# Smaller broadcasts of C in a fused Mamba and local-attention kernel: four 2 KB tiles with their own lead beside five 4 KB tiles for B

## The chip, the core and the metric

The kernel runs on one NeuronCore of one Trainium2 chip. A core has engines that run at the same time, each through its own list of instructions in the order in which the program was written: TensorE (PE, with its weight loads PEld), VectorE (DVE), ScalarE (ACT), GpSimd (POOL) and SyncE (SP), which here does nothing but issue DMAs. Engines wait for one another by semaphores. The metric is device time in microseconds of the whole kernel; lower is better.

## What is computed

The input x is 4096 tokens of 256 features. Two branches start from it and their results are added to x.

- A Mamba block: project the normalised x to 512 channels twice (x_inner and a gate z), a causal convolution of 4 taps and silu on x_inner, then a selective scan with 16 states for each channel, and an output projection.
- A local transformer of two layers: attention over windows of 128 tokens that also look at the window before, 8 heads of 64, and a gated MLP of width 682.

The part that the change touches is the scan. For each channel d, state n and token l:

```
dt  = softplus(dt_lr @ dt_proj_w.T + dt_proj_b)
dA  = exp(dt[d] * A[d, n])
dBx = dt[d] * x_conv[d] * B_ssm[l, n]
h   = dA * h + dBx
y  += h * C_ssm[l, n]
```

B_ssm and C_ssm are rows of 16 states that are the same for all channels. Everything is in 32-bit floats.

## The kernel before

Channels lie on the 128 partitions and tokens along the free axis. The Mamba branch goes in 8 blocks of 512 tokens (`NB`), each with 4 groups of 128 channels (`CI`) and 16 states; the transformer branch goes in 16 steps of 256 tokens (`ST`) for each of the two layers. Both are interleaved through the whole kernel: 32 MLP steps stand beside 32 pairs of block and channel group.

`recur(b, c, g)` (from L775) handles two states (`NG = 2`) of one block and channel group; there are 256 such calls, 512 states in all. In the kernel before, one call

- takes two tiles of the pool `spreads` (L381: 7 tiles, 128 x 1024, 4 KB in each partition) and issues for each a DMA of 512 KB that broadcasts two rows of B, or two rows of C, from DRAM to all 128 partitions;
- multiplies the B tile, u, by dt*x on POOL (L793), one instruction of 1024 columns for both states;
- for each state: ACT makes the decay exp(dt*A) in one of two PSUM tiles (L802), DVE scans (L807), ACT keeps the last column as state (L813), DVE multiplies the scan by the row of C into u (L817);
- in every second call POOL adds the two states (L825), and PE transposes the result and sums it in PSUM (L829, tile y). When all 16 states are in, `close` copies y (L846), turns it back (L850), and DVE and POOL finish the channel group (L854, L859).

So the tile u is held from its DMA until PE has read it, and the C tile from its DMA until the second product on DVE.

The block's front comes earlier: `in_proj` (PE, L635), a copy and a scaled copy on ACT (L665, L672), three taps for each channel group on DVE (L678), silu, the small projection `front_dbl` (PE L702, result to DRAM by SP), then `times` (PE L734) and `prepare` (the softplus on ACT, DVE and POOL, L742 to L770).

In the transformer branch `load_rest` brings the MLP weights of a layer. It lets PE make a bias out of them (`shift`, L495), and DVE adds that bias (L506, L507) and scales the weights (L511). An MLP step ends with the gelu on ACT (L1213, with a table load on each side), products on POOL (L1221), and the down projection on PE (L1247 in layer 0, L1266 in layer 1). `finish` adds the result to a tile of sums (L546).

What sets the order is a planner in the kernel itself. Each `add` records an operation with its engine, a supposed duration and a lead, `soon`; a lower key (time wanted less `soon`) goes first. `Plan.order` plays the operations through and writes every engine's instructions in the order that comes out. Once written, the order is fixed: an instruction that is not ready holds up all that stand behind it on its engine, DMA issues on SP among them. PE's `part` tells whether a matmul uses the whole array, row halves (`rows`) or column halves (`columns`).

Of the kernel before, what the change touches and what calls it, by code (L numbers as in the profile page):

```python
# [42 lines left out]
AHEAD = 2.32  # L43
# [275 lines left out]
def mamba_and_local_transformer(  # L319
# [61 lines left out]
    spreads = buffer("bc", 7, [P, NG, TB])  # L381
# [73 lines left out]
    def load_small():  # L455
        dma(96, lambda: xpw.ap, lambda: xp_wT.rearrange("(c p) n -> p c n", p=P), writes=[xpw], soon=-0.84)
        for at_row in (0, DH):
            dma(32, lambda at_row=at_row: dtw.ap[at_row : at_row + DTR], lambda: dt_wT, writes=[(dtw, at_row)], soon=-0.13)
        dma(128, lambda: b2row.ap, lambda: b2_d[DEPTH - 1 : DEPTH, :].partition_broadcast(P), writes=[b2row], soon=-0.82)

    def load_qkv(l):
        for s in range(3):
            cut = slice(s * INNER, (s + 1) * INNER)
            dma(
                512, lambda cut=cut: wqkv.ap[:, :, cut],
                lambda cut=cut: wqkv_d[l][:, cut].rearrange("(k p) n -> p k n", p=P), writes=[(wqkv, s)], soon=-0.17,
            )

    def load_rest(l):
        dma(512, lambda: wo.ap, lambda: wo_d[l].rearrange("(h p) n -> p h n", p=P), writes=[wo], soon=0.41)  # L470
        for half in range(2):
            for m, n in ((0, WHOLE), (NM - 1, LAST)):
                to, of = w1_at(half, m), half * HID + m * MC
                dma(
                    n, lambda to=to, n=n: w1.ap[:, :, to : to + n],
                    lambda of=of, n=n: w1_d[l][:, of : of + n].rearrange("(k p) n -> p k n", p=P),
                    writes=[(w1, (half, m))], soon=-1.5,
                )
# [3 lines left out]
            lambda: w2_d[l][0:whole, :].rearrange("(m p) n -> p m n", p=MC), writes=[(w2, 0)], soon=0.34,  # L482
        )
        dma(42, lambda: w2.ap[0 : HID - whole, NM - 1, :], lambda: w2_d[l][whole:HID, :], writes=[(w2, 1)], soon=0.91)
# [28 lines left out]
        add("PE", 8.3, shift, [w1], [pb], soon=-0.76)  # L513
        add("DVE", 0.4, bias, [pb], [b1, b1x], soon=-0.11)
        add("DVE", 4.6, scale, [], [w1], port=True, soon=-1.45)
# [14 lines left out]
    def base_of(s):  # L530

        base = plan.value(rows_b)
        if s in sums:
            dma(256, lambda: base.ap, lambda: sums[s].ap, [sums[s]], [base], soon=-0.77)
            return base
        dma(256, lambda: base.ap, lambda: rows(x, s), writes=[base], soon=-1.13)
# [3 lines left out]
            ), [b2row], [base], soon=-0.58,  # L540
# [3 lines left out]
    def finish(s, po, base):  # L544

        add("DVE", 0.6, lambda: nc.vector.tensor_tensor(base.ap, halves(po), base.ap, ALU.add), [po], [base], soon=-1.06)  # L546
        if s in sums:
            dma(256, lambda: rows(out, s), lambda: base.ap, [base], soon=-0.55)
            return
        sums[s] = plan.fixed(dram.tile([P, NW, D], F32, tag=f"sum{s}", name=f"sum{s}"))  # L550
        dma(256, lambda: sums[s].ap, lambda: base.ap, [base], [sums[s]], soon=-1.4)
# [4 lines left out]
    def shift_column(l, s):  # L556
        now = xts[l, s]
        if s == 0:
            add("POOL", 0.14, lambda: nc.gpsimd.memset(now.ap[:, 1, 0:1], 0.0), [], [(now, 0)], soon=-0.51)
        else:  # L560
# [3 lines left out]
                [(old, 1)], [(now, 0)], soon=-0.73,  # L564
            )

    def normalize(s):
# [5 lines left out]
        dma(256, lambda: xb.ap, lambda: rows(x, s), writes=[xb], soon=0.15)  # L573
# [27 lines left out]
        add("DVE", 1.1, stats, [xb], [mv], soon=1.5)  # L601
        add("ACT", 0.5, root, [mv], [rstd], soon=0.26)
        add("DVE", 0.6, centre, [mv, rstd], [xb], port=True, soon=0.02)
        now = xts[0, s] = plan.value(tokens)
        add("PE", 0.44, turn, [xb], [pt], holds=[now], soon=0.92)
        add("ACT", 0.48, lambda: nc.scalar.copy(now.ap[:, :, 1:], halves(pt)), [pt], [(now, 1)], soon=0.26)
        shift_column(0, s)
        dma(256, lambda: xn_d[s].ap, lambda: now.ap[:, :, 1:], [(now, 1)], [xn_d[s]], soon=0.98)
# [3 lines left out]
    def reload(s):  # L612
        now = xts[1, s] = plan.value(tokens)
        dma(256, lambda: now.ap[:, :, 1:], lambda: x1_d[s].ap, [x1_d[s]], [(now, 1)], soon=0.04)
# [6 lines left out]
    def in_half(i):  # L621
# [3 lines left out]
            lambda: in_wT[:, i * DI : (i + 1) * DI].rearrange("(k p) n -> p k n", p=P), writes=[w], soon=-1.17,  # L625
# [3 lines left out]
    def in_proj(b, w, c, to):  # L629
# [9 lines left out]
        add("PE", 1.72, emit, [w, xms[b]], [pm], holds=[to], soon=-0.68)  # L639
        return pm  # L640

    def front_load(b):
        xm = xms[b] = plan.value(xms_b)
        for i in range(PB):
            s = b * PB + i
            dma(
                256, lambda i=i: xm.ap[:, :, i * TS : (i + 1) * TS], lambda s=s: xn_d[s].ap, [xn_d[s]], [(xm, i)], soon=0.54
# [5 lines left out]
    def front_conv(b, c, w):  # L653
# [4 lines left out]
        else:  # L658
# [3 lines left out]
                [(old, c)], [(xin, 0)], soon=0.95,  # L662
            )
        pm = in_proj(b, w, c, xin)
        add("ACT", 0.48, lambda: nc.scalar.copy(xin.ap[:, TAPS - 1 :], pm.ap), [pm], [(xin, 1)], soon=1.39)  # L665
        if b < NB - 1:
            add(
                "POOL", 0.14, lambda: nc.gpsimd.tensor_copy(tail.ap[:, edge], xin.ap[:, TB:]), [(xin, 1)], [(tail, c)], soon=-0.13
# [5 lines left out]
            ), [], [pm], soon=-1.0,  # L674
# [8 lines left out]
        for j in range(TAPS - 1):  # L683
            add("DVE", 0.7, lambda j=j: tap(j), [xin, pm], [(xc, c) if j == TAPS - 2 else pm], soon=1.04)

    def silu(v):
# [4 lines left out]
        add("ACT", 4.52, emit, [], [v], soon=0.84)  # L691

    def front_dbl(b):
# [3 lines left out]
        def emit():  # L697
# [9 lines left out]
        add("PE", 1.75, emit, [xc, xpw], [px], holds=[xd, part], soon=-0.37, part="columns")  # L707
        add("ACT", 0.48, lambda: nc.scalar.copy(part.ap[0:n, 0:TB], px.ap[DH : DH + n]), [px], [part], alone=[px], soon=-0.04)
        add(
            "DVE", 0.6, lambda: nc.vector.tensor_tensor(xd.ap[0:n], px.ap[0:n], part.ap[0:n, 0:TB], ALU.add),  # L710
            [px, part], [(xd, 0)], alone=[px], soon=-1.5,
        )

        add("ACT", 0.48, lambda: nc.scalar.copy(xd.ap[DH : DH + DTR], xd.ap[0:DTR]), [(xd, 0)], [(xd, 1)], soon=-0.52)
        xds[b] = xd
        bc = bcs[b] = plan.fixed(dram.tile([2 * NS, TB], F32, tag=f"bc{b}", name=f"bc{b}"))
        dma(64, lambda: bc.ap, lambda: xd.ap[DTR:n, :], [(xd, 0)], [bc], soon=-0.16)

    def gate_conv(b, c, w):
# [4 lines left out]
        add("ACT", 0.48, lambda: nc.scalar.copy(sz.ap[:, c, :], pz.ap), [pz], [(sz, c)], soon=-1.5)  # L724

    def times(b, c):
# [12 lines left out]
        add("PE", 1.15, emit, [xd, dtw], banks2, holds=dts2, soon=1.25, part="rows")  # L739
        for i in range(2):  # L740
# [3 lines left out]
                ), [banks2[i]], [dts2[i]], soon=0.16,  # L744
# [3 lines left out]
    def prepare(b, c):  # L748

        if c % 2 == 0:  # L750
# [7 lines left out]
        add("ACT", 0.6, lambda: nc.scalar.activation(e.ap[:, n], dt.ap, AF.Abs), [dt], [e], soon=-0.49)  # L758
        add("ACT", 0.6, lambda: nc.scalar.activation(dt.ap, dt.ap, AF.Relu), [], [dt], soon=-1.5)
        add("ACT", 0.54, lambda: nc.scalar.activation(e.ap[:, n], e.ap[:, n], AF.Exp, scale=-1.0), [], [e], soon=0.5)  # L760
        add(
            "DVE", 0.36, lambda: nc.vector.tensor_scalar(r.ap[:, n], e.ap[:, n], 1.0, -1.0, ALU.add, ALU.add),
            [e], [r], port=True, soon=-0.19,
        )
        add("POOL", 1.22, lambda: nc.gpsimd.tensor_tensor(r.ap[:, n], e.ap[:, n], r.ap[:, n], ALU.subtract), [e], [r], soon=-0.36)
        add("ACT", 0.6, lambda: nc.scalar.activation(e.ap[:, n], e.ap[:, n], AF.Ln, bias=one_t), [], [e], soon=-0.3)
        add("POOL", 1.22, lambda: nc.gpsimd.tensor_tensor(dt.ap, dt.ap, r.ap[:, n], ALU.add), [r], [dt], soon=-1.41)
        add("POOL", 1.22, lambda: nc.gpsimd.tensor_tensor(dt.ap, dt.ap, e.ap[:, n], ALU.add), [e], [dt], soon=-0.94)
        add(
            "DVE", 0.61, lambda: nc.vector.tensor_tensor(dtx.ap, dt.ap, xc.ap[:, c, :], ALU.mult),  # L770
            [dt, (xc, c)], [dtx], port=True, soon=0.7,
# [3 lines left out]
    def recur(b, c, g):  # L775
# [5 lines left out]
        spread = []  # L781
        for s in range(2):
            w = plan.value(spreads)
            dma(
                512, lambda w=w: w.ap.rearrange("p n t -> p (n t)"),
# [636 lines left out]
```

## Time and profile before

| What | Value |
|---|---|
| Median of three runs | 1888.05 us (1886.05 to 1889.43) |
| Profiled execution, its own time | 1890.55 us |
| Its span, first to last instruction | 1888.8 us |
| Mean granted TensorE clock | 0.992 of full speed |
| First matmul starts, last matmul ends | 7.51 us, 1884.84 us |
| Matmul records | 12,432 |
| DMA issues on SP that broadcast B or C | 512 of 512 KB each |

Shares and waits are taken from this one profiled execution. The page counts an engine as busy while any of its instructions runs; matmuls overlap in the pipeline and their ends are modelled, so PE's busy share says little about how much room is left. The distance from one matmul's start to the next one's start says more. In the lists of waits, the columns are the total in microseconds, the number of waits, and the longest.

### The profile page before, as it was taken

To read this page: it belongs to the slowest core of one execution; us is meant where nothing else is said; L and a number is where in the kernel's file an instruction comes from. 1 tells how busy PE (TensorE), PEld (TensorE's weight loads), DVE (VectorE), ACT (ScalarE), POOL (GpSimd) and SP (SyncE) were. 2 spreads that over 40 slices of the span, in tenths; PEclk is the share of its full clock that TensorE was granted. 3 is DMA by queue.
4 is the path that set the end of the run, shared out by engine and by line. 5 is a ranking of instruction groups with operands and counts; after the bars stand their busy time and mean duration, and the time that the engine had idled before them with its cause. 6 is when DMAs were issued, how large, how long until landed. Compare 5 with 4: busy or idle time off the path is not lost. (4 is left out here: it accounts for less than half of the span.)

```text
span 1888.8 us, 35786 instructions
## 1 busy us (share of the span) xinstructions
PE 1850.9 (98%) x12432; PEld 1422.4 (75%) x12432; DVE 1667.1 (88%) x3030; ACT 1588.7 (84%) x3794; POOL 1508.6 (80%) x1274
## 2 busy tenths in 40 slices
PE   7999999999999999999999999999999999999997
PEld 4777767777777777778778787787778777787886
DVE  6688898899898999988899888989889898899886
ACT  5788888888898888897896979988798888988793
POOL 4578778887887778887888787988788987798885
PEclk9899999999999999999999999999999999999999
DMA  5354555565455555556555554556544575455564
GB/s 189 125 193 131 171 167 167 178 209 179 157 176 190 181 179 185 164 186 208 166 186 204 181 191 147 187 170 209 176 147 171 176 248 169 144 173 175 193 197 142
DMA packets 133956, 334.69 MB, mean 177 GB/s; under 512 B 13468, under 2 KB 57200, under 8 KB 133776
## 3 DMA queue, kind: packets, MB, share of 16 engines
q1 hardware_dynamic: 133488, 332.21, 53.1%
q8 instruction: 98, 1.61, 0.3%
q14 instruction: 82, 0.67, 0.1%
q10 hardware_dynamic: 288, 0.20, 0.0%
HBM read 315.06 MB, written 17.30 MB: 176 GB/s over the span
## 5 line engine op out<-in xcount | busy, mean ns | idle before, releaser
L793 POOL TENSOR_TENSOR bc<-dtx,bc 128x1024 f32<-128x1024 f32 x256 | 605.7, 2368 | 80.7 <-DMA bc<-bc 44.7
L807 DVE TENSOR_TENSOR_SCAN da<-da,state,bc 128x512 f32<-128x512 f32 x448 | 563.7, 1279 | 56.6 <-ACT da L802 32.8
L802 ACT ACTIVATE da<-dt,negA 128x512 f32<-128x512 f32 x512 | 349.2, 698 | 49.7 <-DVE bc L817 47.9
L918 PE MATMUL mm<-wqkv,xt 128*128 128x512 f32 x768 | 353.5, 598 | 1.4 <-DVE top L1032 0.8
L817 DVE TENSOR_TENSOR bc<-da,bc 128x512 f32<-128x512 f32 x512 | 338.3, 679 | 5.8 <-ACT state L813 3.7
L1176 PE MATMUL mm<-hn,w 128*128 128x256 f32 (+1 forms) x1408 | 329.2, 381 | 2.1 <-DVE top L1032 0.7
L1176 PEld LDWEIGHTS mm<-hn,w 128*128 128x128 f32 (+1 forms) x1408 | 256.1, 188 | 39.1 <-DVE top L1032 1.6
L1042 ACT ACTIVATE pr<-pr,top 128x256 f32<-128x256 f32 (+1 forms) x512 | 253.3, 501 | 10.6 <-DVE top L1032 10.4
L918 PEld LDWEIGHTS mm<-wqkv,xt 128*128 128x128 f32 x768 | 139.7, 191 | 137.0 <-issue 121.2
L1032 DVE CUSTOM_DVE_ANT_0 pr<-mm,maskf,nrm 128x256 f32<-128x256 f32 (+1 forms) x512 | 212.4, 473 | 14.5 <-PE mm L1017 13.7
L825 POOL TENSOR_TENSOR bc<-bc 128x512 f32<-128x512 f32 x128 | 165.3, 1291 | 71.5 <-DVE bc L817 65.2
L829 PE MATMUL y<-ident,bc 128*128 128x128 f32 x1536 | 219.6, 277 | 2.2 <-ACT m2k L846 1.5
L985 POOL TENSOR_TENSOR turn<-turn,trig 128x512 f32<-128x512 f32 x128 | 162.4, 1288 | 74.0 <-DVE turn L978 63.0
L829 PEld LDWEIGHTS y<-ident,bc 128*128 128x128 f32 x1536 | 177.1, 141 | 58.6 <-issue 40.0
L945 POOL TENSOR_TENSOR turn<-turn,turn 128x512 f32<-128x512 f32 x128 | 164.2, 1283 | 32.4 <-DVE turn L965 31.4
L1017 PEld LDWEIGHTS mm<-kT,qT 64*128 64x128 f32 x2016 | 119.7, 187 | 30.9 <-issue 21.9
L1221 POOL TENSOR_TENSOR mlp<-mlp,ga 128x512 f32<-128x512 f32 (+2 forms) x128 | 127.2, 1008 | 19.1 <-ACT ga L1233 10.0
L1059 ACT COPY prT<-mm 128x512 f32<-128x512 f32 (+1 forms) x256 | 133.9, 595 | 3.4 <-PE mm L1055 3.1
L1017 PE MATMUL mm<-kT,qT 64*128 64x128 f32 x2016 | 135.4, 280 | 0.0
L1071 PE MATMUL mm<-prT,v 128*64 128x128 f32 x2016 | 134.5, 281 | 0.0
L1071 PEld LDWEIGHTS mm<-prT,v 128*64 128x64 f32 x2016 | 113.8, 137 | 25.1 <-issue 8.8
L1055 PE MATMUL mm<-ident,pr 128*128 128x128 f32 x1008 | 130.5, 276 | 2.0 <-ACT qT L956 0.9
(132 smaller groups left out, 3499.4 us busy)
## 6 DMA issues: line engine op xcount, KB each, us to landing
bc<-bc SPq DMA_DIRECT2D x512, 512.0 KB, 4.5
io<-in_x SPq DMA_DIRECT2D x32, 256.0 KB, 5.4
mw<-in_in_wT SPq DMA_DIRECT2D x16, 512.0 KB, 4.8
rot<-in_rot SPq DMA_DIRECT2D x32, 128.0 KB, 4.2
xn<-xt SPq DMA_DIRECT2D x16, 256.0 KB, 3.6
xm<-xn SPq DMA_DIRECT2D x16, 256.0 KB, 4.4
x<-mid SPq DMA_DIRECT2D x16, 256.0 KB, 4.6
mw<-in_out_wT SPq DMA_DIRECT2D x8, 512.0 KB, 6.1
```

The lines of the kernel that those rows point to most:

```text
L793: "POOL", 2.35, lambda: nc.gpsimd.tensor_tensor(u.ap, dtx.ap.unsqueeze(1).to_broadcast([P, NG, TB]), u.ap, ALU.mult), [dtx], [u], soon=-0.28,
L802: "ACT", 0.63, lambda h=h, n=n: nc.scalar.activation(h.ap, dt.ap, AF.Exp, scale=negA[:, c * NS + n : c * NS + n + 1]), [dt], [h], soon=0.0,
L807: "DVE", 1.18, lambda h=h, n=n, i=i: nc.vector.tensor_tensor_scan(h.ap, h.ap, u.ap[:, i, :], state.ap[:, c, n : n + 1] if b else 0.0, ALU. ...
L817: "DVE", 0.61, lambda h=h, i=i: nc.vector.tensor_tensor(u.ap[:, i, :], h.ap, spread[1].ap[:, i, :], ALU.mult), [h, spread[1]], [(u, i)], a ...
L825: add("POOL", 1.22, lambda: nc.gpsimd.tensor_tensor(u.ap[:, 0, :], u.ap[:, 0, :], u.ap[:, 1, :], ALU.add), [], [u], soon=-1.1)
L829: nc.tensor.matmul(y.ap[:, t, :], lhsT=u.ap[:, i, t * P : (t + 1) * P], rhs=ident, is_transpose=True, start=g == 0 and i == 0 and t == 0, ...
L918: nc.tensor.matmul(pm.ap, lhsT=hT[k], rhs=wqkv.ap[:, k, q * INNER : (q + 1) * INNER], start=k == 0, stop=k == KC - 1,)
L1017: nc.tensor.matmul(halves(scs[j])[:, i, a * WIN : (a + 1) * WIN], lhsT=qT.ap[half, 2 * g + i, :], rhs=kk.ap[half, 2 * g + i, :], start=n == 0,
L1032: nc.vector.tensor_tensor_reduce(out=prs[j].ap[:, i, keys], in0=halves(scs[j])[:, i, keys], in1=mask[:, keys], scale=nrm.ap[:, h : h + 1], ...
L1042: nc.scalar.activation(prs[j].ap[:, i, keys], prs[j].ap[:, i, keys], AF.Exp, bias=top.ap[:, h : h + 1], scale=-1.0, accum_out=den.ap[:, h ...
L1071: nc.tensor.matmul(hpair(po.ap)[j * DH : (j + 1) * DH, hp, :], lhsT=vv.ap[:, h * DH : (h + 1) * DH], rhs=prT.ap[:, j, a, :], start=a == first,
L1176: nc.tensor.matmul(halves(pm)[0:r, i, :], lhsT=w1.ap[:, k, c0 : c0 + r], rhs=hn.ap[:, k, :], start=k == 0, stop=k == KC - 1,)
```

## The change

The pool `spreads` shrinks from seven tiles to five and serves B alone. A new pool `readouts` of four tiles of 128 x 512 (2 KB in each partition) serves C. A call of `recur` issues one DMA of 512 KB for B and, for each of its two states, one DMA of 256 KB for C. The bytes in SBUF (28 KB in each partition) and the bytes moved stay as they were. The leads `soon` of nearly all operations, and the planner's horizon `AHEAD`, have other values; the DMA of B now has the lead -0.14 and that of C -1.5, where both had -0.76. No operation of an engine other than SP is added or taken away, but the order of the instructions on every engine is another one.

```diff
-AHEAD = 2.32
+AHEAD = 2.34
...
-    spreads = buffer("bc", 7, [P, NG, TB])
+    spreads = buffer("bc", 5, [P, NG, TB])
+    readouts = buffer("cc", 4, [P, TB])
...
-        add("PE", 8.3, shift, [w1], [pb], soon=-0.76)
-        add("DVE", 0.4, bias, [pb], [b1, b1x], soon=-0.11)
-        add("DVE", 4.6, scale, [], [w1], port=True, soon=-1.45)
+        add("PE", 8.3, shift, [w1], [pb], soon=-1.41)
+        add("DVE", 0.4, bias, [pb], [b1, b1x], soon=0.06)
+        add("DVE", 4.6, scale, [], [w1], port=True, soon=0.25)
...
         y, bc = ys[b, c], bcs[b]
-        spread = []
-        for s in range(2):
-            w = plan.value(spreads)
-            dma(
-                512, lambda w=w: w.ap.rearrange("p n t -> p (n t)"),
-                lambda s=s: bc.ap.rearrange("(s n) t -> s n t", s=2)[s, g * NG : (g + 1) * NG, :]
-                .rearrange("n t -> (n t)").partition_broadcast(P), [bc], [w], soon=-0.76,
-            )
-            spread.append(w)
-
-        u = spread[0]
+        rows_of = lambda s, n, k: bc.ap.rearrange("(s n) t -> s n t", s=2)[s, n : n + k, :].rearrange("n t -> (n t)").partition_broadcast(P)
+        u = plan.value(spreads)
+        dma(512, lambda: u.ap.rearrange("p n t -> p (n t)"), lambda: rows_of(0, g * NG, NG), [bc], [u], soon=-0.14)
...
         for i in range(NG):
             n = g * NG + i
+            cc = plan.value(readouts)
+            dma(256, lambda cc=cc: cc.ap, lambda n=n: rows_of(1, n, 1), [bc], [cc], soon=-1.5)
...
-                "DVE", 0.61, lambda h=h, i=i: nc.vector.tensor_tensor(
-                    u.ap[:, i, :], h.ap, spread[1].ap[:, i, :], ALU.mult
-                ), [h, spread[1]], [(u, i)], alone=[h], soon=-0.32,
+                "DVE", 0.61, lambda h=h, i=i, cc=cc: nc.vector.tensor_tensor(
+                    u.ap[:, i, :], h.ap, cc.ap, ALU.mult
+                ), [h, cc], [(u, i)], alone=[h], soon=-0.25,
...
-        add("ACT", 0.48, lambda: nc.scalar.copy(ytv(), y.ap), [y], [yt], soon=-0.43)
+        add("ACT", 0.48, lambda: nc.scalar.copy(ytv(), y.ap), [y], [yt], soon=-0.7)
...
-        add("PE", 0.44, turn, [yt], [py], soon=-0.55)
+        add("PE", 0.44, turn, [yt], [py], soon=0.51)
...
-        add("ACT", 4.1, gelu, [], [u], soon=-1.49)
+        add("ACT", 4.1, gelu, [], [u], soon=-1.33)
```

## The prediction

> **What bounds the kernel now.** I read the page first, then the chain of waits, the stages, the lists of waits, and the two ends of the timeline.
>
> ```profile
> span 1888.8 us, 35786 instructions
> ...
> PE 1850.9 (98%) x12432; PEld 1422.4 (75%) x12432; DVE 1667.1 (88%) x3030; ACT 1588.7 (84%) x3794; POOL 1508.6 (80%) x1274
> ```
>
> PE at 98% may only mean that matmuls overlap. The chain tells what PE needs at full pace, where matmuls follow one another without a wait:
>
> ```profile
> 1665.33 3.57 PE mm L1112 x32
> 1669.33 1.73 PE mm L1176 x8
> ...
> 1678.83 1.72 PE mm L918 x4
> ...
> 1693.96 1.95 PE mm L1071 x32
> ...
> 1701.24 1.99 PE mm L1017 x32
> ```
>
> Per matmul this is 430 ns for 512 columns, 216 for 256, 111 for 128 (109 where weights don't change), 61 where two halves of the array work at once (L1071; 56 for L1017 by its starts). The instruction counts times these: 1024 x 0.43 = 440, 2560 x 0.216 = 553, 4592 x 0.1095 = 503, 2016 x 0.0555 = 112, 2016 x 0.061 = 123, small forms 39: near 1,766 us with unrounded starts. So 118 us of PE's time up to its last matmul (1884.84) are lost, and the change keeps all 12,432 matmuls. Where is it lost? Setting each matmul's start against the sum of work before it: 7.6 us before the first; 19.2 us at 39 us of work; 23.8 at 61; 46.9 at 300; 107.5 at 1750; 118.3 at the end. From 300 to 1750 it is 60.6 us in 1450, 4.2 in 100, of which most is inherent: of 1,313 changes from one group of matmuls to the next, 1,076 cost under 0.1 us and 27 us in all, and each turn to the row halves about 0.2. I put true waits there at 10 us. What a better order can win lies at the ends:
>
> ```profile
> 0.00:300.00 300.00, 280.81 (x1824) 203.97 (x1825) 244.72 (x485) 241.68 (x582) 212.42 (x214) 0.98 0.50 163
> 300.00:600.00 300.00, 298.41 (x1992) 228.28 (x1991) 278.12 (x517) 259.58 (x643) 248.79 (x207) 1.00 0.53 175
> ...
> 1800.00:1889.00 89.00, 76.20 (x506) 65.92 (x504) 63.89 (x89) 54.89 (x113) 61.74 (x43) 0.95 0.52 172
> ```
>
> PE (first column after the length) is idle for 19 us in the first stage, 13 in the last, 1.6 between. What the tiles of B and C do stands in the waits:
>
> ```profile
> POOL bc L793 <- DMA bc<-bc: 44.7, 33, 3.6
> ...
> DVE da L807 <- POOL bc L793: 12.6, 10, 4.2
> ```
>
> POOL waits 44.7 us for B. No line shows DVE's second product (L817) waiting for C. Following every tile from its DMA to its last reader: B is used a median 1.4 us after it lands, C 9.4 us after; B is held 29.7 us on average (median), C 17.8. A call of recur comes every 1889/256 = 7.38 us, so seven tiles offer 51.6 us and are filled for 47.5: C's slack is bought with B's.
>
> **The change part by part.** *B's tiles.* Five tiles for B alone offer 5 x 7.38 = 36.9 us against 29.7 held, so B can be asked for some 7 us earlier and most of the 44.7 us go. They are POOL's; POOL has 20% idle, and only 12.6 us reach the scan. On PE, waits that POOL ends cost 17 us in all, 9 of them at the end of the kernel. So I take -4.5, between 0 (all hidden) and -10.
>
> *C's tiles.* A tile is free when DVE has ended L817 and is used again four states later. In the new program DVE's own work between the two, at the durations of this trace, is at least 5.8 us, below 7 in 5 of 508 cases, below 8 in 25, with a median of 12.5. Landings: 4.5 us for the 512 KB, 4.4 for 256 KB from DRAM (xm<-xn); the slowest tenth of the broadcasts took over 6.2 us, the slowest 10. Before, SP issued within 0.1 us of the tile's release in nine of ten cases, though its queue is in order and nearly always waits (DVE 645 us, PE 499 us), so releases come in the order in which the DMAs stand. About one use in forty is late by about 1 us: 13 us on DVE, which has 12% idle: +0.5, between 0 and +3. Behind a late C wait the next scans, POOL's sum and PE's collection.
>
> *More DMAs.* 256 more issues at 0.32 us are 82 us of SP, which waits more than 1,500 us: nothing, while releases stay in order. [...] I take the trace: 0.
>
> *The start.* In both programs the first block's chain is conv, silu, L702, L734, softplus, first scan, first collection (L829). Before:
>
> ```profile
> 51.64 6.87 PE L495 MATMUL mm<-cols,w 128*128 128x1 f32 x48
> ...
> 58.44 2.08 PE L734 MATMUL mm<-xd,dtw 16*128 16x512 f32 x4
> ...
> 84.56 1.09 PE L829 MATMUL y<-ident,bc 128*128 128x128 f32 x8
> ```
>
> The bias matmuls stand right ahead of L734, whose input was ready at 52.1: it lost 6 us; and from L734 to the first collection it took 24 us, with POOL serving the second channel group's softplus first. The new program has L495 at 15.6 us of PE work (33.8 before), L734 at 41.9 (39.2) and the first collection at 58.1 (60.9); POOL goes straight from the first softplus to L793. New on the chain: the bias and scale of the weights (0.5 + 1.8 us by L506 to L511) stand ahead of the taps on DVE. L495 now needs w1 early: its DMAs come after some 5.1 MB, and 6.2 MB had moved by 22 us before, so it lands near 19, ahead of the 27 to 29 at which PE gets there. I get L734 at 56 to 58, and the chain to the collection needs at least 13 us by its rows (ACT 3 x 0.63, DVE 0.43 + 0.66, POOL 1.38 + 1.27 + 1.27 + 2.37, scans and product 3.1, signals) and more with company, 15 to 18: at 73 to 76, with 58.1 of work done, 15 to 18 us lost where 23.8 were. I take -6, between -10 and +2 (chain as slow as before).
>
> *The end.* Before:
>
> ```profile
> 1857.20 1.28 ACT L1213 ACT_TABLE_LOAD   x1
> ...
> 1862.38 2.47 DVE L807 TENSOR_TENSOR_SCAN da<-da,state,bc 128x512 f32<-128x512 f32 x2 [2.56 <-ACT da L802]
> ...
> 1866.19 2.46 DVE L807 TENSOR_TENSOR_SCAN da<-da,state,bc 128x512 f32<-128x512 f32 x2 [0.16 <-ACT da L802]
> ...
> 1871.32 0.69 DVE L817 TENSOR_TENSOR bc<-da,bc 128x512 f32<-128x512 f32 x1
> ```
>
> After the last gelu begins ACT still has 5 decays to make; two states take 3.81 us, and from the gelu to the last product it is 14.8 us, then 17 us of closing that stay. The new ACT list has 7 decays there: +3.81; three short copies instead of one stand ahead of the first decay: +0.75; and L546 (0.69) stands ahead of the last product: 5.3 in all. PE comes to this gelu with one collection less done (-0.44): +5, between +2 and +7.
>
> *Tighter hand-offs.* The new PE list puts less work between steps that depend on one another through ACT: between the last collection of a channel group and its transposes (L850), under 2.5 us in 12 of 32 groups (2 before); between turning the softmax and mixing (L1055, L1071), under 1.25 us in 19 of 128 (6 before). Without cover the first costs PE 0.84 us (at 1873.5), the second about 0.3 (L1071 waits 6.4 us in 29 for ACT). Most still have 0.9 us or more between: +2, between 0 and +13. Turns between array parts fall from 361 to 351, at 0.1 to 0.2 each: -1.
>
> Sum: -4.5 + 0.5 - 6 + 5 + 2 - 1 = -4. The profiled execution took 1890.55 (1.75 outside its span), so 1886.5 there; the median of the runs is 2.5 lower: 1884.
>
> **The rivals.** *The hand-offs decide, slower:* ACT is 84% busy and works in order, so a copy behind exps or a gelu (4.1 us) comes late, and PE with its fixed list stands. 10 closes at 0.8 and 13 mixes at 0.4 are 13 instead of 2: +7, 1895. It turns the sign from 6 us on. For it: PE has nothing else to do at such a place. Against it: before, such places cost little. *The start heals further:* from 61 to 300 us of work PE lost 23 us, 9.7 in 100; at the later rate it would be 10: 13 less, 1871. For it: B's tiles run short there too. Against it: these waits are on DVE's attention steps. *It does nothing on PE:* B's waits were covered (0), the start gives 3 and the end takes 5: 1889.
>
> **How the numbers follow.** The likeliest, 1884 (own range 1878 to 1890), has 0.47; the hand-offs 0.30; the healed start 0.13; nothing 0.10. A measurement tells about 0.2%, 3.8 us: faster is below 1884.3, slower above 1891.8. Of the likeliest 0.26 is faster, 0.16 same, 0.05 slower; of the hand-offs 0.29 slower; of nothing 0.06 same, 0.02 each side. With the healed start: faster 0.41, same 0.23, slower 0.36. The range leaves out half of the healed start and the hand-offs at their worst: 1872 to 1898.
>
> **What would show it.** Right: POOL's wait for B under 15 us, no wait of L817 for C above 15 us in all, the first collection before 77 us, the last product 19 to 21 us after the last gelu begins, PE's loss from 300 to 1750 us of work between 55 and 62. Wrong: L817 waiting long for cc (C late), L495 waiting for w1, the first collection after 82 us, or a new list of PE waits for ACT at L850 and L1071 of over 8 us.

## The result and the profile after

| | Before | After |
|---|---|---|
| Median on the same chip | 1888.74 us (1886.05 to 1891.51) | 1913.3 us (1911.62 to 1918.26) |
| Ratio, 95% interval | | 1.0134 (1.0110 to 1.0158) |
| Profiled execution, span | 1888.8 us | 1909.8 us |
| Granted TensorE clock | 0.992 | 0.989 |
| PE's time lost, start to last matmul | 118.3 us | 139.3 us |

The change costs 25 us where a gain of 4 was forecast. The last row is counted as in the prediction: each matmul's start less the work that stands before it. The page of the profile after:

```profile
span 1909.8 us, 36533 instructions
...
PE 1859.5 (97%) x12432; PEld 1427.1 (75%) x12432; DVE 1689.1 (88%) x3030; ACT 1589.3 (83%) x3794; POOL 1505.7 (79%) x1274
```

These are the same matmuls and DVE instructions as before, but DVE is busy 22 us longer. Where PE stands still shows first in the table by stages; of before:

```profile
300.00:1000.00 700.00, 695.66 (x4665) 533.57 (x4664) 644.28 (x1184) 609.58 (x1488) 574.79 (x480) 1.00 0.55 181
1000.00:1800.00 800.00, 798.24 (x5443) 618.96 (x5441) 714.20 (x1275) 682.59 (x1615) 659.65 (x540) 1.00 0.54 180
```

and of after (columns: the stretch, then busy time of PE, PEld, DVE, ACT, POOL, then the clock, the DMA share, GB/s):

```profile
300.00:1000.00 700.00, 685.96 (x4622) 525.47 (x4621) 642.47 (x1142) 597.34 (x1448) 561.79 (x473) 1.00 0.55 176
1000.00:1800.00 800.00, 799.72 (x5441) 621.42 (x5438) 718.01 (x1280) 682.58 (x1628) 656.53 (x539) 0.99 0.56 181
```

From 300 to 1000 us, the transformer's first layer, PE idles 14 us instead of 4; from 1000 to 1800 the two are alike. By work done: up to 61 us of work PE has lost 23.7 us (23.8 before); from 61 to 300, 24.0 (23.1); from 300 to 1000, 50.2 (33.9); from 1000 to 1750, 26.2 (26.7); behind that 15.2 (10.8). So of the 21 us, 16.3 fall in layer 0 and 4.4 at the end.

The waits of POOL in the profile after:

```profile
POOL turn L981 <- DVE turn L974: 96.2, 33, 7.4
...
POOL bc L787 <- DMA bc<-bc: 43.2, 31, 4.5
```

The wait for B, which five own tiles were to take away, is still there: 43.2 us, 44.7 before. The new order asks for the tiles so that each is held 36.1 us (median), which is all that five tiles offer (5 x 1909.8/256 = 37.3). And POOL waits half as long again for DVE's rotation (96.2 us; 63.0 before, at L985).

No wait of PE names a DMA of B or C as what ended it. Two places in layer 0 show what does, both of after. The first:

```profile
371.06 1.28 ACT L689 ACT_TABLE_LOAD   x1
...
372.36 1.91 ACT L689 ACTIVATE sz<-sz 128x2048 f32<-128x2048 f32 x1
...
374.29 1.28 ACT L690 ACT_TABLE_LOAD   x1
374.42 0.60 PE L1051 MATMUL mm<-ident,pr 128*128 128x128 f32 x4
...
376.34 1.08 ACT L1055 COPY prT<-mm 128x512 f32<-128x512 f32 x2
...
377.08 0.63 PE L946 MATMUL mm<-ident,turn 128*128 128x128 f32 x4 [2.06 <-ACT prT L1055]
```

PE turns the softmax (L1051) and next needs a bank that ACT empties (L1055). ACT is inside a silu with a table load on each side, 4.5 us, and does two small steps more; PE, whose list is fixed, stands 2.06 us. And more is lost than this wait. Right behind it the granted clock (the third number from the end) is at half for 3.4 us:

```profile
377.90:381.30 3.40, 3.40 (x10) 2.69 (x9) 2.14 (x4) 3.37 (x13) 0.07 (x1) 0.51 0.06 23
381.30:384.70 3.40, 3.40 (x27) 2.69 (x27) 1.81 (x3) 1.81 (x6) 3.40 (x4) 1.00 0.08 30
```

The 13 matmuls of 256 columns that follow (L875) take 4.66 us, where 13 x 0.216 = 2.8 would do. A second spell of 3.4 us at half clock stands behind waits of 1.66 and 0.66 us, from 968.4 us on. In before, neither is there. The second place:

```profile
647.13 3.48 DVE L590 TENSOR_SCALAR io<-io,mv,rstd 128x256 f32<-128x256 f32 x2
...
648.11 4.69 POOL L787 TENSOR_TENSOR bc<-dtx,bc 128x1024 f32<-128x1024 f32 x2
...
650.52 1.28 DVE L803 TENSOR_TENSOR_SCAN da<-da,state,bc 128x512 f32<-128x512 f32 x1
...
652.64 1.38 PEld L1172 LDWEIGHTS mm<-hn,w 128*128 128x128 f32 x7 [2.92 <-DVE top L1028]
652.64 1.56 PE L1172 MATMUL mm<-hn,w 128*128 128x256 f32 x6 [2.51 <-DVE top L1028]
```

Two normalisations on DVE (L590), at most 0.41 us each in the ten cases in which POOL does nothing beside them, take 3.48 us while POOL works, mostly on B; the masks (L1028) behind them are late, and PE stands 2.5 us. (No half clock follows here: it is 1.00 from 652 to 660 us, as it is behind a wait of 1.25 us that ends at 785.7. What brings the spells no run shows.) The planner supposes 0.6 us for both normalisations and keeps them clear of POOL as one block (`port=True`); in the run L787 starts between the two.

Over the whole stretch from 300 to 1750 us of work, PE's waits for other engines rose from about 9.2 to 19.9 us: for ACT from 2.4 to 8.6, for DVE from 3.9 to 6.0, for POOL from 2.9 to 5.3. What matmuls lost at half the clock rose from about 2.3 to 8.0 us: besides the two spells of 3.4 us, the one at the second set of bias matmuls is 10.2 us long instead of 6.8.

### The profile page after: what moved, and what is told of

Read it like the earlier page. It is cut to its first block, busy times and chain, and to the rows that moved or that the text cites. A ratio compares the mean times of both kernels' runs of the same rounds, so it can differ in the third digit from the quotient of the medians.

```text
span 1909.8 us, 36533 instructions
## 1 busy us (share of the span) xinstructions
PE 1859.5 (97%) x12432; PEld 1427.1 (75%) x12432; DVE 1689.1 (88%) x3030; ACT 1589.3 (83%) x3794; POOL 1505.7 (79%) x1274
## 3 DMA queue, kind: packets, MB, share of 16 engines
q1 hardware_dynamic: 170352, 332.23, 54.3%
## 4 chain that ended last, share of the span: by engine, by line
PE 80%; DVE 7%; ACT 5%; POOL 3%; issue 2%; DMA 2%; SPq 0%; DVEq 0%; POOLq 0%; ACTq 0%
PE mm L914 14%; PE mm L1172 13%; PE y L825 8%; PE mm L1067 6%; PE mm L1013 6%; PE mm L1108 5%; PE mm L636 5%; PE mm L1051 5%; PE mm L1262 4%; PE mm L875 3%; PE mm L1243 3%; PE mm L946 2%; DVE da L803 2%; PE mm L1093 1%; PE mm L1137 1%
## 5 line engine op out<-in xcount | busy, mean ns | idle before, releaser
L787 POOL TENSOR_TENSOR bc<-dtx,bc 128x1024 f32<-128x1024 f32 x256 | 604.9, 2368 | 75.2 <-DMA bc<-bc 43.2
L803 DVE TENSOR_TENSOR_SCAN da<-da,state,bc 128x512 f32<-128x512 f32 x448 | 563.4, 1278 | 46.1 <-ACT da L798 30.5
L813 DVE TENSOR_TENSOR bc<-da,cc 128x512 f32<-128x512 f32 x512 | 339.0, 677 | 6.2 <-ACT state L809 3.2
L981 POOL TENSOR_TENSOR turn<-turn,trig 128x512 f32<-128x512 f32 x128 | 161.5, 1284 | 96.2 <-DVE turn L974 96.2
L825 PEld LDWEIGHTS y<-ident,bc 128*128 128x128 f32 x1536 | 176.9, 141 | 60.6 <-issue 32.9
L1028 DVE CUSTOM_DVE_ANT_0 pr<-mm,maskf,nrm 128x256 f32<-128x256 f32 (+1 forms) x512 | 213.5, 472 | 7.5 <-PE mm L1013 6.2
L1217 POOL TENSOR_TENSOR mlp<-mlp,ga 128x512 f32<-128x512 f32 (+2 forms) x128 | 127.5, 1009 | 26.8 <-ACT ga L1229 13.5
L1055 ACT COPY prT<-mm 128x512 f32<-128x512 f32 (+1 forms) x256 | 135.8, 597 | 9.9 <-PE mm L1051 9.7
L809 ACT COPY state<-da 128x1 f32<-128x1 f32 x448 | 71.1, 168 | 87.0 <-DVE da L803 77.4
L1051 PE MATMUL mm<-ident,pr 128*128 128x128 f32 x1008 | 131.1, 274 | 3.9 <-ACT mlp L1187 1.7
L1067 PE MATMUL mm<-prT,v 128*64 128x128 f32 x2016 | 133.6, 279 | 0.5 <-ACT prT L1055 0.5
```

Of the source, the lines that this page charges most:

```text
L787: "POOL", 2.35, lambda: nc.gpsimd.tensor_tensor(u.ap, dtx.ap.unsqueeze(1).to_broadcast([P, NG, TB]), u.ap, ALU.mult), [dtx], [u], soon=-0.9,
L803: "DVE", 1.18, lambda h=h, n=n, i=i: nc.vector.tensor_tensor_scan(h.ap, h.ap, u.ap[:, i, :], state.ap[:, c, n : n + 1] if b else 0.0, ALU. ...
L813: "DVE", 0.61, lambda h=h, i=i, cc=cc: nc.vector.tensor_tensor(u.ap[:, i, :], h.ap, cc.ap, ALU.mult), [h, cc], [(u, i)], alone=[h], soon=- ...
L825: nc.tensor.matmul(y.ap[:, t, :], lhsT=u.ap[:, i, t * P : (t + 1) * P], rhs=ident, is_transpose=True, start=g == 0 and i == 0 and t == 0, ...
L1028: nc.vector.tensor_tensor_reduce(out=prs[j].ap[:, i, keys], in0=halves(scs[j])[:, i, keys], in1=mask[:, keys], scale=nrm.ap[:, h : h + 1], ...
L1051: nc.tensor.transpose(ppv()[:, j, a, :], prs[j].ap[:, i, a * WIN : (a + 1) * WIN], ident)
```

## The experiments

Three theories stood at the start. T1: the loss lies in the newly drawn order of the engines. T2: it lies in the tiles (more and smaller DMAs, B or C late). T3: an order loses whenever it is drawn again without a search over its leads. Ratios below are to the kernel before on the same chip, with 95% intervals. Where "the plan" is named, it is the end that the kernel's own `Plan.order` works out for its list, in its own supposed durations; that is arithmetic of the kernel, not a measurement.

### The tiles under the old order

**e1_halves**: only C's DMA cut in two, old tiles, old order.

```diff
-            dma(512, lambda w=w: w.ap..., lambda s=s: ..., [bc], [w], soon=-0.76)
+            def load(w=w, s=s):
+                for a, k in ((0, NG),) if s == 0 else ((0, 1), (1, 1)):
+                    nc.sync.dma_start(w.ap[:, a : a + k, :]..., ...[s, g * NG + a : g * NG + a + k, :]...)
+            add("SP", 0.32, load, [bc], [w], late=512, soon=-0.76)
```

> The order and the seven shared 4 KB tiles of the kernel before; only each C broadcast goes out as two DMAs of 256 KB into the two halves of the same tile, so 224 more DMAs and issues on SP, and nothing else. If more and smaller DMAs cost the time by themselves (the tiles' theory, T2): 1900 us or more. If what cost is the newly drawn order of the engines (T1): as before, 1886 to 1891. The third theory, that any redrawn order loses against a searched one (T3), says the same as T1 here.

Measured: 0.9999 (0.9990 to 1.0008), 1889.05 us. The run issued 768 broadcasts instead of 512, so 256 more and not 224. More and smaller DMAs cost nothing there.

**e2_old_order_split**: the plan runs with seven tiles as before and fixes the order; the DMAs are then placed anew.

```diff
-    spreads = buffer("bc", 7, [P, NG, TB])
+    spreads = Buffer([None] * 7)
+    tiles_b = [work.tile([P, NG, TB], ...) for i in range(5)]
+    tiles_c = [work.tile([P, TB], ...) for i in range(4)]
```

> The order of every instruction on PE, DVE, ACT and POOL is that of the kernel before; B comes into five tiles of 4 KB, C by single states into four of 2 KB, and each of these DMAs is issued where the plan says that its tile comes free (two B pairs near the end, for which the old order needs a sixth tile, go into the tile of the block's input that nothing uses any more). So it is the tiles' part of the change alone. T1 (the order costs, not the tiles): 1880 to 1892, layer 0 (300 to 1000 us) loses no more PE time than before. T2 (smaller tiles, more DMAs, late B or C): 1900 to 1913, with POOL waiting for B or DVE for C in layer 0. T3: as T1.

Measured: 1.0003 (0.9994 to 1.0011), 1890.48 us. Its waits of POOL:

```profile
POOL bc L861 <- DVE bc L853: 72.2, 38, 6.5
POOL turn L1021 <- DVE turn L1014: 69.7, 33, 4.3
...
POOL bc L829 <- DMA bc<-bc: 20.4, 12, 4.0
```

The wait for B fell from 44.7 to 20.4 us, as the tiles allow. Nothing came of it: POOL waits 7 us longer in each of the two lines above it (65.2 and 63.0 before), for DVE. By work done, PE lost 4 us less than before up to 300 us and 3 us more from 300 to 1000. So here the tiles neither cost nor bring anything in all, T2 falls for this order, and so does the gain that was forecast.

### Leads and tiles apart

**f_newleads_pairs** and **f_oldleads_split**, both planned anew:

```diff
-    spreads = buffer("bc", 5, [P, NG, TB])
-    readouts = buffer("cc", 4, [P, TB])
+    spreads = buffer("bc", 7, [P, NG, TB])
```

and, from the kernel before, the reverse with every old lead kept.

> All leads and the planner's horizon of the changed kernel, but the seven shared tiles of 4 KB and C by pairs as before (C's DMA with B's lead); the planner draws the order anew. T1 in its plain form (the new leads draw a worse order): 1905 to 1915. T2 (the tiles cost): at most 1892. T3 (an order that wasn't searched with its tiles loses, whichever leads it has): 1895 to 1930, and then the run with old leads on new tiles loses as well.

> All leads and the horizon of the kernel before, with the five 4 KB and four 2 KB tiles of the change, C by single states with C's old lead; the planner draws the order anew. T1 in its plain form (the new leads are to blame): 1885 to 1893. T2 (the tiles): 1905 or more. T3: 1895 to 1930, worse than either kernel or between them, together with the run with new leads on old tiles.

Measured: 1.0385 (1.0364 to 1.0405), 1962.32 us, and 1.0255 (1.0236 to 1.0273), 1936.06 us. Both lose more than the whole change, and more than the 1895 to 1930 us that T3 gave. The loss can't be split into a part of the leads and a part of the tiles in this way: leads fit one set of tiles. That is T3's mechanism, with a larger cost than it named. (With the old tiles C's DMA has B's new lead, so not quite all leads are those of after.)

### Does the time follow the plan?

**h_split_searched** and **h_pairs_searched** have the tiles of after and of before. Their leads and `AHEAD` were varied at random and kept where the plan's end came down; **g_after_ahead232** has one line changed.

```diff
-AHEAD = 2.34
+AHEAD = 2.32
```

> The tiles of the change (five of 4 KB, four of 2 KB, C by single states), with other leads: they were drawn until the kernel's own planner put its end at 1889.6 us by its own clock; it puts the changed kernel's at 1895.7 and that of the kernel before at 1882.4. If the loss is the drawn order's (T1): it moves with the plan, about 6 us under the changed kernel at least, 1895 to 1908. [...] The tiles' theory fell with the run that kept the old order; it would say 1910 or more.

> The seven shared tiles and C by pairs of the kernel before, with other leads, drawn until the planner put its end at 1875.6 us, 6.8 us under the kernel before's own plan. T1: it follows the plan and beats the kernel before, 1878 to 1888. If what lies outside the plan decides: 1885 to 1905, since this order, unlike that of before, gives no assurance about hand-offs that the plan doesn't know.

> The changed kernel with the planner's horizon back at 2.32; the order drawn is the same over the first 1500 us of TensorE's work and differs only behind that, where the plan idles TensorE 4.8 us longer. T1 (the time follows the drawn order's own holes): 4 to 6 us slower than the changed kernel, 1916 to 1921. If chance outside the plan decides: 1908 to 1925, either side of it.

| Kernel | Plan's end | Measured | Measured less plan |
|---|---|---|---|
| before | 1882.4 | 1888.74 | 6.3 |
| after | 1895.7 | 1913.3 | 17.6 |
| h_pairs_searched | 1875.6 | 1890.32 | 14.7 |
| h_split_searched | 1889.6 | 1897.63 | 8.0 |
| g_after_ahead232 | 1900.5 | 1924.63 | 24.1 |
| f_oldleads_split | 1917.2 | 1936.06 | 18.9 |
| f_newleads_pairs | 1931.8 | 1962.32 | 30.5 |

The ratios are 0.9998 (0.9989 to 1.0007) for h_pairs_searched, 1.0044 (1.0029 to 1.0059) for h_split_searched, 1.0172 (1.0158 to 1.0186) for g_after_ahead232. The time follows the plan in its rough course, but 6 to 31 us come on top that the plan doesn't know. The kernel before has the least on top. h_split_searched has the very tiles of after and is 0.90% or 17 us faster than it: so much at least is the order's. But T1 has only half of its size from the plan: 13 of the 25 us are in the plan of after, and some 11 are not. g_after_ahead232 lost 0.38% or 7 us to after by the ratios, near the 4 to 6 expected (11 us by the medians, on another chip), but h_pairs_searched missed its 1878 to 1888: a step of some microseconds in the plan foretells nothing exactly.

### What comes on top: stretched DVE work

The small instruction on DVE that clamps the squared norms from below writes the tile nrm. In before and in after (minimum, median, maximum in ns):

```profile
L972 DVE TENSOR_SCALAR nrm<-nrm x64: 116/164/3507, 16.5 to 1804.2; 128x16 f32<-128x16 f32 x64
```

```profile
L968 DVE TENSOR_SCALAR nrm<-nrm x64: 152/167/4039, 16.6 to 1817.1; 128x16 f32<-128x16 f32 x64
```

An instruction of 0.17 us that now and then takes 4. All 64 took 22.2 us before and 35.7 after. In after the 36 with no work of POOL beside them took at most 0.175 us, the 28 others 0.94 in the median; in before the 41 without took at most 0.174, the 23 others 0.33 in the median. It was taken out of both:

```diff
-        add("DVE", 0.08, lambda: nc.vector.tensor_scalar_max(nrm.ap, nrm.ap, NORM_MIN**2), [], [nrm], port=True, soon=0.35)
+        add("DVE", 0.08, lambda: None, [], [nrm], port=True, soon=0.35)
```

> The changed kernel with its order kept, less the 64 small VectorE instructions that clamp the squared norms from below (tensor_scalar_max on nrm): the kernel leaves that clamp out. They took 35.7 us of DVE there, against 22.2 us in the kernel before, because some of them stand still while GpSimd works. If such unplanned stretches of DVE cost the loss in layer 0: 1913 less 8 to 20, so 1893 to 1905, and more is gained than by the same cut in the kernel before. If the order drawn holds the loss in its own hand-offs: at most 6 us less, 1907 to 1913, and about as much as in the kernel before.

> The kernel before with its order kept, less the same 64 clamps (left out). The stretched DVE theory: 0 to 4 us less, 1885 to 1890, so clearly less than what the changed kernel gains. The theory that the drawn order itself holds the loss: the same gain in both, whatever it is.

Measured: 1.0093 (1.0076 to 1.0110), 1906.43 us, and 0.9986 (0.9978 to 0.9995), 1887.89 us. After gains 0.41% or 7.7 us, before 2.6. By these values both theories missed, the first narrowly: 5 us of the change's loss are the stretched clamp. The intervals are wide, though, 2 to 13 us for the 7.7; a second pair further down (0.39%) bears the size out, and the two together give about 5 us, give or take 4. In layer 0 of the profiled executions PE lost 3.5 us less without the clamp, and at half the clock 4.4 us instead of 8.0: there the gain is about what the clock no longer loses. For a kernel that keeps a floor, ScalarE's logarithm that follows can carry it:

```diff
-            nc.scalar.activation(nrm.ap, nrm.ap, AF.Ln, scale=65536.0)
+            nc.scalar.activation(nrm.ap, nrm.ap, AF.Ln, scale=65536.0, bias=eps_t)
...
-        add("DVE", 0.08, lambda: nc.vector.tensor_scalar_max(nrm.ap, nrm.ap, NORM_MIN**2), [], [nrm], port=True, soon=0.1)
+        add("DVE", 0.08, lambda: None, [], [nrm], port=True, soon=0.1)
```

> The order, tiles and leads of the kernel before; the clamp of the squared norms is no instruction of VectorE any more but a small bias in ScalarE's logarithm that follows it (the floor under a norm becomes about 1e-5 instead of 1e-12). As the run of the kernel before that leaves the clamp out: 1886 to 1889, 0.05 to 0.2% faster than before. If the gain there was chance: 1888 to 1891.

> The order that the planner ends at 1875.6 us on the old tiles, which took 1890 with stretched clamps, with the clamp as the same bias in ScalarE's logarithm. If unplanned stretches of DVE are what keeps this order from following its plan: it gains more than the kernel before does, 1882 to 1887, and beats both kernels. If not: 2 us as there, 1887 to 1890.

Measured: 0.9988 (0.9980 to 0.9996), 1888.77 us, and 0.9951 (0.9937 to 0.9964), 1882.84 us. The order that was 7 us better in its plan now shows it: it is the fastest kernel that computes everything, and beats both. In its list of waits:

```profile
POOL turn L985 <- DVE turn L978: 68.1, 28, 5.8
POOL bc L793 <- DMA bc<-bc: 64.0, 49, 4.3
```

The fastest kernel is one in which POOL waits 20 us longer for B than in before and after. (The two slowest, f_newleads_pairs and f_oldleads_split, have 88.0 and 83.6.) How long POOL waits for B does not tell the end.

### The tiles under a third order, and under after's own

**fold_searched_split** puts the tiles of the change under this fastest order, by nearly the same edit as e2. (Two of B's loads find no free tile before the plan wants their product to start; they stand there and make it late.)

> The fastest order so far (searched leads, clamp as a bias, 0.9951 of the kernel before, where GpSimd waits 64 us for B) with the engines' order kept and the tiles of the change under it: B into five of 4 KB, C by single states into four of 2 KB, each DMA where its tile comes free (one late B pair goes into the dead tile of the block's input). If GpSimd's wait for B is on no path that sets the end (T1): its wait falls to under 35 us and the time stays within 0.2% of that order's, 0.993 to 0.997 of the kernel before. If the tiles are worth what was forecast once the order has long waits for B: 4 to 9 us less, 0.990 to 0.993. If smaller DMAs cost after all: above 0.998.

Measured: 1.0063 (1.0049 to 1.0077), 1900.65 us. By the ratios this is 1.0063 - 0.9951 = 1.1% or 21 us slower than the same order on seven shared tiles (18 by the medians). Of the three outcomes named, the last one came: the smaller tiles cost after all. In the timeline:

```profile
1316.98 2.35 POOL L833 TENSOR_TENSOR bc<-dtx,bc 128x1024 f32<-128x1024 f32 x1 [2.30 <-DMA bc<-bc]
...
1319.28 1.26 POOL L985 TENSOR_TENSOR turn<-turn,turn 128x512 f32<-128x512 f32 x1
...
1320.60 0.42 PEld L990 LDWEIGHTS mm<-ident,turn 128*128 128x128 f32 x4 [2.99 <-POOL turn L985]
1320.60 0.66 PE L990 MATMUL mm<-ident,turn 128*128 128x128 f32 x4 [2.76 <-POOL turn L985]
```

Here is the path by which a late B does reach PE: behind the product that waits for B stands the sum of a rotated query (L985) on POOL's list, and PE's next step needs it. PE's waits for that sum are 13.6 us in all, 2.4 on the seven tiles. POOL's wait for B even fell, to 52.4 us, but in 24 waits instead of 49: fewer and longer. No line shows DVE waiting for C. Two runs part the causes; both read C from one tile that is loaded once, and so leave out the other transfers of C.

```diff
-    tiles_b = [work.tile([P, NG, TB], ...) for i in range(5)]
-    tiles_c = [work.tile([P, TB], ...) for i in range(4)]
+    tiles_b = [work.tile([P, NG, TB], ...) for i in range(6)]
+    tiles_c = [work.tile([P, TB], ...) for i in range(1)]
```

> As the run that put the change's tiles under the fastest order (1.0063 of the kernel before), with B in five tiles, but C is read from one tile that is loaded once; the other 511 transfers of C are left out. If B's fifth tile being too few costs the 18 us there: no gain from this, 1894 to 1902, TensorE's turns still waiting over 8 us for GpSimd. If C's many small DMAs, which share SP's queue with B's, make B late: 1880 to 1886.

> The same, with six tiles of 4 KB for B. If the number of B's tiles is the cause: 1878 to 1885, with GpSimd's waits of over 3 us for B gone. If C's DMAs were the cause: as the run with five tiles, whichever that takes.

Measured: 0.9980 (0.9971 to 0.9988), 1886.97 us with five, and 0.9955 (0.9937 to 0.9972), 1881.1 us with six. So C's transfers cost 0.83% or 16 us there, the lack of a sixth tile 0.25% or 5 us: both causes have a part. PE's waits for the sum fell with them, from 13.6 to 6.3 and 1.3 us. B landed in a median of 4.67 us with C's transfers and 4.13 without, and SP issued within 0.1 us of the release of the tile at the median in both, so it is later landing more than a blocked queue. Whether C's bytes or the number of its DMAs make B late, no run under this order tells. With six tiles POOL has no long wait for B left, and the time is that of the seven shared tiles, whose 64 us of short waits cost nothing.

Now the same three steps under after's own order.

> The changed kernel with its order kept on PE, DVE, ACT and POOL and five tiles for B; C is read from one tile that is loaded once, the other 511 transfers of C are left out. If C's single transfers make B or C late in this order: 8 us or more under the changed kernel (1.0134 of the kernel before), to below 1.009. If the order's own holes and the stretched clamps hold the loss: 1.009 to 1.014.

> The same with six tiles of 4 KB for B, so that B comes a call earlier. GpSimd's wait for B (43 us in the changed kernel) should nearly vanish. If the tiles hold the loss: 1.000 to 1.006 of the kernel before. If the order drawn holds it: 1.007 to 1.013; by its plan, which ends 13 us after the plan of the kernel before, 1.007 is left whatever B and C do.

> As the run before it, and the clamp of the norms is a bias in ScalarE's logarithm: no wait for B, no C transfers, no stretched clamps. What is left is the order drawn. By the difference of the two plans 13 us over the kernel before less the 2 us that the clamp costs there: 1.004 to 1.008. If it gets to 1.002 or less, the drawn order itself is not to blame.

Measured: 1.0103 (1.0088 to 1.0118), 1909.84 us; 1.0126 (1.0109 to 1.0143), 1913.82 us; 1.0087 (1.0071 to 1.0102), 1906.94 us. In the second, POOL's waits:

```profile
POOL turn L1007 <- DVE turn L1000: 104.2, 36, 7.4
...
POOL bc L813 <- DMA bc<-bc: 1.1, 1, 1.1
```

B's wait is gone, 43.2 to 1.1 us, and the ratio went from 1.0134 to 1.0126, inside the intervals; POOL waits for DVE instead. (Five tiles without C's transfers took 0.31% less than after, at the edge of the intervals; six take most of that back, and nothing here explains this step.) With the clamp folded away as well, 1.0087 remain, just above the 1.004 to 1.008 expected. Against fold_before, which has the old order and the same fold, that is 1.0087 - 0.9988 = 0.99% or 18.7 us, with no B wait, no C transfer and no clamp: it is in the order drawn, with all that this order brings about. The long PE waits there, all but the fourth as in after:

```profile
PE y L851 <- DVE bc L839: 6.6, 3, 5.6
PE y L851 <- POOL bc L847: 4.1, 2, 3.4
PE mm L1198 <- DVE top L1054: 3.1, 3, 2.1
PE mm L972 <- DVE top L1054: 3.0, 3, 1.6
PE mm L972 <- ACT prT L1081: 2.9, 1, 2.9
```

The first two are the end; the last is the silu of 371 us, and the third the place at 649 us, where the two normalisations still take 3.05 us.

So the 25 us are: about 19 by the order drawn (13 of them already in its plan; the interval is 3 us either way), about 5 by the clamps, which take longer beside POOL's work in this order (35.7 us in all, 22.2 before), and about 1 by B and C (1.5 us by the run with six tiles, 6 by the one with five, within the intervals and at their edge). Open is why the plan of after is worse than that of before. Its own durations put 2 us of the 13 before 300 us of work, 7 between 300 and 1000 and 4 at the end. The five and four tiles didn't force all of it, since h_split_searched has them and a plan 6 us shorter; whether they forced the rest is open: the searches ended at 1889.6 with the new tiles and 1875.6 with the old. Nor is it shown what the other 5 to 6 of the 19 us are that the plan doesn't hold; the stretched normalisations, with 2.1 us of PE's waiting, are one piece. Between these two kernels it is not the clock: both ran at 0.991 in the mean of their runs. Between before and after the clock has its part, as the result shows.

## Why the prediction was wrong

By its terms, in the profiled executions: B's tiles -4.5, measured 0; C +0.5 and more DMAs 0, measured nothing clear; the start -6, measured -0.1; the end +5, measured +4.4; tighter hand-offs and turns +2 - 1, measured +15.8. With 0.9 us more between 61 and 300 us of work this is 21 us, where -4 was forecast. The step that failed above all is "Tighter hand-offs": it was sized by two kinds of places, and the loss came at others.

**The hand-offs** (+2) are the term that turned the sign: PE's loss from 300 to 1750 us of work rose from 60.6 to 76.4 us. The mechanism was named rightly, copies on ACT that stand behind a long function while PE waits with a fixed list. But PE's true waits there, put at 10 us before (9.2 by the trace), about doubled, and only 6 of the 11 us that they grew end on ACT. The other 6 us or so of the 15.8 are matmuls at half the clock, for which the prediction had no term. Nor had it one for DVE's instructions that take longer beside POOL's work, although these are behind waits such as the one at 652.6 us. The rival "the hand-offs decide" put 13 us on this term (+7 in its sum). That its 13 came near 15.8 is luck: it put 8 us on the closes and 5 on the mixes, and PE's waits at these two (L846, L1067) are 1.0 and 0.5 us in after. An order over 9,000 operations, drawn anew, was judged by two of its pairs.

**The start** (-6) failed: 23.7 us lost against 23.8. The bias matmuls did move, to 27.5 us, but there they stand ahead of the projection that feeds the convolution (L636):

```profile
27.47 7.54 PE L496 MATMUL mm<-cols,w 128*128 128x1 f32 x48
...
34.93 9.60 PE L636 MATMUL mm<-xm,mw 128*128 128x512 f32 x16
...
50.28 1.91 ACT L689 ACTIVATE xc<-xc 128x2048 f32<-128x2048 f32 x1
...
62.62 1.13 PE L735 MATMUL mm<-xd,dtw 16*128 16x512 f32 x4
...
81.76 0.66 PE L825 MATMUL y<-ident,bc 128*128 128x128 f32 x4
```

The projection begins 7.2 us later than before (27.77), and it takes 9.60 us where its two pieces took 5.42 and 1.88: the half clock that stands behind the start of the bias matmuls (29.7 to 39.9 us) now falls on it. So the silu begins 7.8 us later than before (42.52), L735 4.2 us later than L734 did and not at 56 to 58, and the first collection comes at 81.8, between the marks set for right and wrong. The seven microseconds taken out of one place of the chain had been put into another place of the same chain; I followed only the place that they left. The rival of a start that heals further failed too: from 61 to 300 us of work PE lost 24.0 us instead of 23.1.

**B's tiles** (-4.5) failed twice. The wait of POOL under 15 us that was named as the sign did not come, since the new order filled the tiles again. And where the wait fell, nothing was gained in these two orders: 20.4 us in e2, 1.1 in m6_after_one_c. (Under the third order a sixth tile was worth 5 us.) The error was to take a share of POOL's wait over to PE. POOL had other waits, for DVE, right behind it, and the prediction had itself found that most of B's wait is POOL's alone.

**C** (+0.5) **and the number of DMAs** (0) were about right for the old order and for this one: DVE hardly waits for C (0.6 us by name), which is used 8.1 us after it lands (median), e1_halves shows nothing (0.9999 with 256 DMAs more), the SP queue's share of the DMA engines is 54.3% (53.1 before; a packet of 4 KB took 159 ns in the median and one of 2 KB 84, in both), and leaving C's transfers out under after's order gave 0.31%. As a general rule the step would have been wrong: under the third order C's transfers cost 16 us, with B landing 0.54 us later beside them.

**The end's** +5 was right. From the last gelu to the last product it took 1892.60 - 1872.09 = 20.5 us, within the 19 to 21 named, and PE lost 4.4 us more there than before:

```profile
1872.09 1.28 ACT L1209 ACT_TABLE_LOAD   x1
...
1892.60 0.69 DVE L813 TENSOR_TENSOR bc<-da,cc 128x512 f32<-128x512 f32 x1
```

## What to carry to other kernels

An engine's wait is worth what stands behind it on its own list and who needs that; its sum alone tells little (64 us of waits for B in the fastest kernel, 1.1 us in one that is 1.3% slower than the kernel before). More than a wait itself can be lost behind it: in after, 2.06 us of PE's waiting were followed by 3.4 us at half the clock, and 2.51 us at another place by none. A change that redraws a fixed order of all engines has to be judged by the order, and the way to part it from the rest is to keep the old order and put only the new resource under it. Where leads have been fitted to one set of tiles, changing either alone can cost more than any effect that was to be measured.

## What was not expected of the hardware

Some instructions on DVE that read only SBUF took longer in after while POOL worked: a clamp of 128x16 4.04 us, where the 36 with no work of POOL beside them took at most 0.175, and two normalisations 3.48 instead of 0.8. Others did not: the sums of squares (L927), which read only SBUF too, took at most 0.69 us with POOL's work beside them and without. DVE's other products beside the same POOL work, with one operand in PSUM (L813), took at most 0.693. What tells these instructions apart, no run shows. A small instruction also took longer than one of POOL's: the clamp of 4.04 us, at 952.6 us in after, stood while two of L1217 and an L787 of 2.35 us between them went by.

The granted clock falls to 0.74 in the 20 us around the bias matmuls, in which PE is hardly idle:

```profile
20.00:40.00 20.00, 19.06 (x92) 13.16 (x91) 13.25 (x36) 8.97 (x29) 10.72 (x16) 0.74 0.41 131
1020.00:1040.00 20.00, 20.00 (x119) 15.34 (x117) 19.10 (x33) 10.38 (x25) 18.58 (x16) 0.74 0.51 183
```

The half clock begins 2.2 us after the first of them and lasts 10.2 us (29.7 to 39.9). In before the same happens at both sets, from 54.6 to 64.8 us and from 1017.1 to 1023.9. No run changes these matmuls, 48 of one column in 7.5 us, so what brings the clock down there is not shown.
